# A two-layer graph network on one core: the inverse transform moved into the group in front, the state difference kept in h's tile, the aggregation in four tiles of the array

## The chip, the cores and the metric

The kernel runs on one core of a Trainium2 chip. The metric is the device time in microseconds of one execution, as the median of several runs. Lower is better. Beside it there is one profiled execution with a trace of every instruction; its page gives a span, which is a little shorter than the device time of that same execution.

The engines are named as in the profile: PE is TensorE (PEld its weight loads), DVE is VectorE, ACT is ScalarE, POOL is GpSimd and SP is SyncE, which here only issues DMAs. A name such as L735 is a line of the kernel file before the change.

## What is computed

The input x has 128 graphs of 128 nodes with 256 features, adj has 128 matrices of 128 x 128. All is fp32. Two layers run one after another, each on the normalized and rectified x, and each adds to x:

```python
h = jnp.maximum(_layernorm(x, axis=-1), 0.0)
x = x + _L0_gnn_ref(h, adj, ...)
h = jnp.maximum(_layernorm(x, axis=-1), 0.0)
x = x + _L1_gnn_ref(h, adj, ...)
```

Layer 0 takes h through a convolution branch (a 1x1 convolution, a convolution of 17 taps over the nodes, batch norms, and a sum with h), through a message branch, and then through a gated cell:

```python
x_conv = relu(bn2(conv2(relu(bn1(conv1(xc))))) + xc)      # xc is x transposed
x_nmp = einsum('bnm,bmd->bnd', A, relu(x @ w_msg.T + b_msg))
gi = concatenate([x_conv, x_nmp], -1) @ w_ih.T + b_ih
gh = x @ w_hh.T + b_hh
r = sigmoid(gi_r + gh_r)
z = sigmoid(gi_z + gh_z)
nn_ = tanh(gi_n + r * gh_n)
return (1.0 - z) * nn_ + z * x
```

Layer 1 works on the first 25 nodes only. For five groups of these nodes (25, 9, 7, 6 and 6 nodes, 53 rows together) it runs two graph convolutions and adds the weighted results:

```python
support = einsum('bnd,de->bne', x, W)
out = relu(einsum('bnm,bme->bne', norm_adj, support) + b)
```

## The kernel before

**Tiling.** Four graphs are a group; there are 32 groups q. Sixteen graphs, that is four groups, are a block of layer 1; there are 8 blocks. Activations of a group are kept with features on the partitions, as [128, 2, 512]: two halves of the features, four graphs of 128 nodes.

**Stages.** Up to about 680 us the first stages run: the 1x1 convolution and a Fourier transform of it (stage_a), products in the Fourier domain (stage_b, results in DRAM as yd), and beside them the message branch (early, results in DRAM as xmd). h itself also waits in DRAM, as hTd. Then stage_c handles the groups one by one: it applies the inverse Fourier transform, forms x_conv, and runs the gates. Beside stage_c, as its groups become ready, run layer 1's rows (second normalization), prepare (the normalized adjacency of a block, ac, and its transposed form r4) and block (the two graph convolutions).

**Order of the work.** The order of instructions on every engine is fixed when the program is built. Each stage is a generator that yields a cost and a delay in microseconds; Order.run picks among lanes by the cost that each has been charged, relative to its weight. Costs and delays only arrange instructions; on the chip each engine runs its own instructions in that order and waits on semaphores. Groups run two at a time in their lane, so that the tail of a group falls into the next one.

**stage_n (L677)** loads hT and xm of a group, as soon as the group two before has issued its last gate product. hT has three buffers, xm two.

**stage_c (L687), the start.** For each of two halves h of the group, 16 matmuls (L706) with four column tiles of 32 apply the inverse to yt (80 frequencies) and write pi, in ptmp; VectorE transposes pi in blocks into xi (L711); the next group's yt is requested (L713); for two feature halves VectorE multiplies xi by a scale and adds hT into xc (L716) and ScalarE adds a shift and rectifies (L719). xi shares a buffer with the later sums tc.

**The gates.** A product is written as seven smaller ones over sums and differences of halves of the weights and of the operands (th, tm and tc are the sums of hT, xm and xc, made on VectorE by L586). part (L730) issues matmuls of one product into a PSUM bank; bank (L744) takes a bank of pgat (three banks) or of ptmp (five). At the start of the gates p1, p6 and p5 are taken; their parts of hT and xm come first (L762 to L764), then p1's part of xc (L765), the copy of p1 into u2 (L766) and the sums tc (L767 to L769). Then follow three products of wh (L781 to L786), a second accumulation into p1 (L788), p6's part of tc (L791), p5's part (L796), sums of the next group (L797), and the products 6 and 3 of z (L803, L810), the second accumulation into p5 (L816), and products with wn (L828 to L853).

**The end of a group.** After the last gate product come two tanh on ScalarE (L855), and on GpSimd, for both feature halves, d = hT - r (L858), d times z (L859) and the sum with r into z (L861). d lies in the buffers of u2 and u3. After a delay of 11 us, in the next group, z is transposed (L878) and added to xt, which has been loaded from x (L809), and the result goes out (L887).

**Layer 1's aggregation.** prepare loads the adjacency of 16 graphs into aj by one DMA (L954), adds the identity (L958), normalizes, and transposes ac by a matmul with the constant e4 (L1001) into r4 (L1005). In ac, two graphs of 64 rows each lie on the 128 partitions. In block, after the dense products, turn (L1064) transposes a group's result into zt, gather (L1075) multiplies it by ac and adds a bias, and fuse (L1086) adds up the node groups. A gather call has four matmuls of 64 x 64 with 256 columns: for graph pair a and half s of the partitions, rows of half s give output rows of the same half s, all in one PSUM tile pg2 of [128, 2, 256].

Of the kernel before, what the change touches and what calls it, by code (L numbers as in the profile page):

```python
# [9 lines left out]
FP = mybir.dt.float32  # L10
AF = mybir.ActivationFunctionType
ALU = mybir.AluOpType
# [3 lines left out]
B, N, D = 128, 128, 256  # L16
# [3 lines left out]
P = 128  # L20
GB = 4
# [9 lines left out]
SB = 16  # L31
# [7 lines left out]
NR = sum(SIZES)  # L39
# [53 lines left out]
def _constants():  # L93

    row_node = [n for g in GROUPS for n in g]
    row_group = [i for i, g in enumerate(GROUPS) for _ in g]
    fwd, inv, tap = _fourier()
    parts = {
        "ident": np.eye(P),
        "mhalf": np.full((P, 8), -0.5),  # L100
        "fwd": fwd, "tap": tap, "inv": inv,
        "ones2": np.kron(np.eye(2), np.ones((RP, RP))),
        "et": np.zeros((P, 2 * RP)),
        "same": np.zeros((P, RP)),
        "diag": np.zeros((P, RP)),
        "e4": np.zeros((P, P)),
        "s2": np.zeros((P, 2 * WIDE)),
        "grp": np.zeros((P, NG)),
        "sgrp": np.zeros((P, 2 * NG)),
        "grpt": np.zeros((P, P)),  # L110
        "sel": np.zeros((P, P)),
        "emb": np.zeros((P, 12)),
    }

    roles = {0: [(2, 2, 0), (0, 0, 1), (1, 1, 0), (0, 0, 1)],
             1: [(0, 0, -1), (0, 0, 1), (1, 1, 0), (1, 1, 0)],
             2: [(1, 1, 0), (1, 1, 0), (0, 0, -1), (0, 0, 1)]}
    for j in range(GB):
        for role, factors in roles.items():
            for ch in range(3):  # L120
                k = WIDE * j + 3 * role + ch
                parts["sel"][ch, k] = 1
                parts["emb"][k] = np.array(factors).T.reshape(-1)
    for r, (n, g) in enumerate(zip(row_node, row_group)):
        for s in range(2):
            k = s * RP + r
            parts["et"][n, k] = 1
            parts["same"][k, [i for i in range(NR) if row_group[i] == g]] = 1
            parts["diag"][k, r] = 1
            for j in (s, s + 2):  # L130
                parts["e4"][k, j * WIDE + n] = 1
            parts["s2"][k, s * WIDE + n] = 1
            parts["grp"][k, g] = 1
            parts["sgrp"][k, s * NG + g] = 1
            parts["grpt"][g, k] = 1
    at, o = {}, 0
    for name, a in parts.items():
        at[name] = (o, o + a.shape[1])
        o += a.shape[1]
    return np.concatenate(list(parts.values()), 1).astype(np.float32), at  # L140
# [67 lines left out]
def kernel(ctx: ExitStack, tc: tile.TileContext, x, adj, consts, vecs, w_se, conv1_w,  # L208
# [380 lines left out]
    def some_sums(q, n):  # L589

        if q in IN:
            if q not in SUMS:
                hT, xm = IN[q]
                (th, a), (tm, b) = sums("th", q, hT), sums("tm", q, xm)
                SUMS[q] = th, tm, a + b
            while SUMS[q][2] and n != 0:
                SUMS[q][2].pop(0)()
                n = n and n - 1
# [85 lines left out]
        yield 0.0, 7.0  # L684
        IN[q] = hT, xm

    def stage_c(q):  # L687
        while not (q - 1 in G_DONE and q in IN):
            yield 0.0, 0.5
        some_sums(q, None)  # L690
        (hT, xm), (th, tm, _) = IN.pop(q), SUMS.pop(q)

        if (q, 0) not in IN2:
            load_yt(q, 0)
            load_yt(q, 1)
            yield 0.0, 6.0
        fr = LATE["co"]
        xi = fr.tile([P, 2, 512], FP, tag="tc", name=f"xi{q}")
        xc = fr.tile([P, 2, 512], FP, tag="xc", name=f"xc{q}")
        for h in range(2):  # L700
            yt = IN2.pop((q, h))
            pi = ptmp.tile([P, 2, 2, 4, WIDE], FP, tag="tmp", name=f"pi{q}_{h}")
            for n in range(4):
                o = n % 2 * WIDE
                for w in range(4):
                    nc.tensor.matmul(  # L706
                        pi[w * WIDE:(w + 1) * WIDE, :, :, n].rearrange("p k g c -> p g k c"),
                        inv[:F, o:o + WIDE],
                        yt[:, n // 2::2].rearrange("f g (k w c) -> w f g k c", k=2, w=4)[w],
                        start=True, stop=True)  # L710
            nc.vector.transpose(xi[:, :, h * D:(h + 1) * D],  # L711
                                pi.rearrange("p k g n c -> p k (g n c)"))
            load_yt(q + 1, h)  # L713
            s = slice(h * D, (h + 1) * D)
            for co in range(2):
                nc.vector.scalar_tensor_tensor(xc[:, co, s], xi[:, co, s],  # L716
                                               scl["bn2"][:, co:co + 1], hT[:, co, s],
                                               op0=ALU.mult, op1=ALU.add)
                nc.scalar.activation(xc[:, co, s], xc[:, co, s], AF.Relu,  # L719
                                     bias=sft["bn2"][:, co:co + 1])  # L720
        yield 1.8, 0.0

        wrz, wn, wh = LATE["wrz"], LATE["wn"], LATE["wh"]

# [34 lines left out]
        r1, r2 = r[:, :, :D], r[:, :, D:]  # L759
        early = [(0, hT, th), (2, xm, tm)]  # L760
        p1, p6, p5 = bank(wrz, 0), bank(wrz, 5), bank(wrz, 4)
        for ps, i in ((p1, 0), (p6, 5), (p5, 4)):  # L762
            part(ps, wrz, i, early, True, False)
            yield 1.75, 0.0  # L764
        part(p1, wrz, 0, xs[2:], False, True)  # L765
        nc.scalar.activation(u2, p1, AF.Copy)  # L766
        tcs, todo = sums("tc", q, xc)  # L767
        for operation in todo:
            operation()  # L769
        yield 0.87, 0.0  # L770
        xs, xh = [(0, hT, th), (2, xm, tm), (1, xc, tcs)], [(0, hT, th)]

        ve = fr.tile([P, 3, 1, D], FP, tag="ve", name=f"ve{q}")
# [22 lines left out]
        part(p5, wrz, 4, xs[2:], False, True)  # L796
        some_sums(q + 1, 2)  # L797
        yield 0.87, 0.0
        while q and q - 1 not in C_DONE:
            yield 0.0, 0.5  # L800
        z = fr.tile([P, 2, 512], FP, tag="z", name=f"z{q}")
# [52 lines left out]
        for dc in (1, 0):  # L854
            nc.scalar.activation(r[:, dc], r[:, dc], AF.Tanh, bias=v("b_ih", 4 + dc))  # L855

            d = fr.tile([P, 512], FP, tag=f"u{2 + dc}", name=f"d{q}_{dc}")
            nc.gpsimd.tensor_sub(d, hT[:, dc], r[:, dc])  # L858
            nc.gpsimd.tensor_mul(d, d, z[:, dc])  # L859
            pat = "p (j t n) -> p t j n"  # L860
            nc.gpsimd.tensor_add(z[:, dc].rearrange("p (t j n) -> p t j n", t=4, j=GB),  # L861
                                 d.rearrange(pat, j=GB, t=4),
                                 r[:, dc].rearrange(pat, j=GB, t=4))
# [83 lines left out]
    def prepare(blk):  # L947

        while not (blk - 1 in P_DONE and blk - 2 in {-2, *B1_DONE}):
# [1 line left out]
        pool, pool2, b1 = S["pool"], S["pool2"], S["b1"]  # L951
        ac, r4 = S["ac"][blk % 2], S["r4"][blk % 2]
        aj = pool.tile([NN, SB, NN], FP, tag="dd", name=f"aj{blk}")
        nc.sync.dma_start(out=aj, in_=adj[blk * SB:(blk + 1) * SB, :NN, :NN]  # L954
                          .rearrange("b n m -> n b m"))
        yield 0.0, 4.0

        for r, n, w in _runs():  # L958
# [43 lines left out]
                         start=True, stop=True)  # L1002
        for j in range(GB):
            s = slice(j * WIDE, (j + 1) * WIDE)
            nc.vector.tensor_copy(r4[s, :, j, :], pr4[s, :, j // 2, :NR])  # L1005
        yield 0.9, 1.0
        P_DONE.add(blk)

    def block(blk):
# [64 lines left out]

        def gather(q):  # L1075
            zt = zts[q]
            pg2 = ptmp.tile([P, 2, D], FP, tag="tmp", name=f"pg2{blk}_{q}")
            for a in range(2):
                for s in range(2):
                    rows = slice(s * RP, (s + 1) * RP)  # L1080
                    nc.tensor.matmul(pg2[rows, a], ac[rows, 2 * q + a], zt[rows, a],  # L1081
                                     start=True, stop=True)
            nc.vector.tensor_tensor(zt, pg2, b2row[:, None, :].to_broadcast([P, 2, D]), ALU.add)
            nc.scalar.activation(zt, zt, AF.Relu)

        def fuse(q):  # L1086
            zt = zts.pop(q)
            pf = ptmp.tile([P, D], FP, tag="tmp", name=f"pfu{blk}_{q}")
            for a in range(2):
                nc.tensor.matmul(pf[a * 2 * WIDE:(a + 1) * 2 * WIDE], s2w, zt[:, a],  # L1090
                                 start=True, stop=True)
            nc.vector.tensor_add(x1[:, q], x1[:, q], pf)
            b0 = blk * SB + q * GB
            if blk < NBLK - 1:
                nc.gpsimd.dma_start(out=out[b0:b0 + GB, :WIDE], in_=x1[:, q])
                return
            for j in range(GB):
                eng = nc.scalar if q == QS - 1 and j % 2 else nc.sync
                eng.dma_start(out=out[b0 + j, :WIDE], in_=x1[j * WIDE:(j + 1) * WIDE, q])

        for what, q in ((turn, 0), (turn, 1), (turn, 2), (gather, 0), (turn, 3), (gather, 1),
                        (gather, 2), (fuse, 0), (gather, 3), (fuse, 1), (fuse, 2), (fuse, 3)):
            what(q)
            if (what, q) == (gather, QS - 1):
                B1_DONE.add(blk)
            yield {turn: 0.45, gather: 0.9, fuse: 0.5}[what], 0.5
        F_DONE.add(blk)


# [70 lines left out]
```

## Time and profile before

| what | value |
|---|---|
| median of 3 runs | 2050.7 us (2047.82 to 2055.25) |
| the profiled execution, device time | 2049.36 us |
| its span | 2047.5 us |
| granted TensorE clock, mean | 0.995 |
| PE busy from 830 to 1936 us | 1098.14 of 1106.00 us |
| DVE, ACT, POOL busy in the same stretch | 754.04, 319.65, 354.70 us |
| aggregation matmuls, L1081 | 34.2 us busy, 256 instructions |
| inverse matmuls, L706 | 62.7 us busy, 2048 instructions |
| GpSimd's d, L858 | 87.2 us busy, 64 instructions |

Busy time of TensorE counts overlapping matmuls once. In lists of groups a row gives busy time, then the mean of one instruction in ns, then the idle time of the engine just before and what ended it. In a timeline a row gives the start, the duration, engine, line, operation and how many instructions were merged into it; a mark in brackets gives idle time before it and what ended that.

### The profile page before, as it was taken

The numbers are of one execution on the slowest core, as the hardware profiler recorded it, in microseconds if no ns is written. First come the engines' busy times: TensorE is split into PE (matmuls) and PEld (weight loads), VectorE is DVE, ScalarE is ACT, GpSimd is POOL, SyncE is SP. The second block draws the span as 40 slices with busy tenths as digits, with TensorE's granted clock in tenths as the row PEclk, the third lists the DMA queues.
The fourth block names the chain that finished last, engine by engine and source line by source line (L and its number), as shares of the span: only waits on it lengthen the run. The fifth ranks groups of instructions, "written<-read, shape, count | busy, mean of one in ns | idle before, by whom it ended". The sixth has DMA issues, their size and how long they took to land.

```text
span 2047.5 us, 34132 instructions
## 1 busy us (share of the span) xinstructions
PE 2006.3 (98%) x12852; PEld 1659.2 (81%) x12852; DVE 1285.1 (63%) x2775; ACT 688.5 (34%) x1547; POOL 741.3 (36%) x898
## 2 busy tenths in 40 slices
PE   7998999999999999999999999999999999999998
PEld 5667888888888888878788788878888888878875
DVE  6774445875433676757756776777567667766742
ACT  4663222454222344222222332232232323222333
POOL 3552665333655032422422233233224323233230
PEclk9999999999999999999999999999999999999999
DMA  9997788645777544431323232332332233323121
GB/s 217 295 284 229 265 267 281 191 162 185 253 256 245 152 127 131 116 108 53 87 73 91 75 84 83 101 80 76 83 88 78 76 98 90 86 78 104 39 71 52
DMA packets 190148, 281.91 MB, mean 138 GB/s; under 512 B 23626, under 2 KB 143375, under 8 KB 189983
## 3 DMA queue, kind: packets, MB, share of 16 engines
q1 hardware_dynamic: 156942, 185.46, 31.7%
q0 software_dynamic: 32656, 93.98, 14.5%
q8 instruction: 102, 1.67, 0.3%
q14 instruction: 64, 0.52, 0.1%
q10 hardware_dynamic: 384, 0.28, 0.1%
HBM read 187.34 MB, written 92.27 MB: 137 GB/s over the span
## 4 chain that ended last, share of the span: by engine, by line
PE 89%; DVE 3%; issue 3%; POOL 3%; DMA 2%; ACT 1%; SPq 0%; POOLq 0%; DVEq 0%; ACTq 0%
PE p L735 39%; PE pa L526 7%; PE pm L630 5%; PE ph L1038 5%; PE pz L1047 5%; PE pc L421 4%; PE pb L526 3%; PE pf L432 3%; PE px L656 3%; PE pi L706 3%; PE pg L1081 1%; PE pw L474 1%; PE po L878 1%; PE ph L410 1%; PE py L1021 1%
## 5 line engine op out<-in xcount | busy, mean ns | idle before, releaser
L858 POOL TENSOR_TENSOR d<-hTc,r 128x512 f32<-128x512 f32 x64 | 87.2, 1362 | 299.3 <-ACT r L855 288.7
L526 PE MATMUL pa<-wf,X 128*128 128x256 f32 x640 | 152.2, 381 | 0.0
L716 DVE SCALAR_TENSOR_TENSOR xc<-xi,s_bn,hTc 128x256 f32<-128x256 f32 x128 | 148.1, 1195 | 2.3
L558 DVE SCALAR_TENSOR_TENSOR y<-pa,kk 128x512 f32<-128x512 f32 x78 | 53.8, 690 | 151.4 <-ACT kk L557 151.4
L887 POOL DMA_DIRECT2D out<-xt x128 | 72.2, 569 | 172.5 <-DVE xt L884 169.3
L750 ACT ACTIVATE z<-z,brz 128x256 f32<-128x256 f32 x128 | 58.1, 501 | 221.3 <-DVE z L804 187.9
L735 PE MATMUL p<-tm,wrz 128*128 128x256 f32 x512 | 132.3, 381 | 0.0
L735 PE MATMUL p<-th,wrz 128*128 128x256 f32 x512 | 132.1, 380 | 0.0
L735 PE MATMUL p<-tc,wrz 128*128 128x256 f32 x512 | 131.8, 380 | 0.0
L526 PEld LDWEIGHTS pa<-wf,X 128*128 128x128 f32 x640 | 118.1, 190 | 16.2 <-issue 2.0
L630 PE MATMUL pm<-wmsg,hT 128*128 128x256 f32 x512 | 123.3, 386 | 0.0
L421 PE MATMUL pc<-c1w,hTa 128*128 128x256 f32 x512 | 121.4, 383 | 1.2 <-ACT hTa L412 1.2
L1040 ACT ACTIVATE hh<-ph,vec 128x96 f32<-128x96 f32 (+3 forms) x160 | 64.4, 403 | 147.0 <-PE ph L1038 137.8
L1038 PE MATMUL ph<-yz,w 128*128 128x96 f32 (+3 forms) x640 | 110.5, 327 | 1.9 <-issue 1.0
L719 ACT ACTIVATE xc<-xc,t_bn 128x256 f32<-128x256 f32 x128 | 64.8, 508 | 138.8 <-DVE xc L716 138.8
L630 PEld LDWEIGHTS pm<-wmsg,hT 128*128 128x128 f32 x512 | 97.3, 193 | 15.8 <-ACT kk L557 1.4
L421 PEld LDWEIGHTS pc<-c1w,hTa 128*128 128x128 f32 x512 | 94.3, 191 | 18.2 <-DVE h L424 4.8
L735 PEld LDWEIGHTS p<-tm,wrz 128*128 128x128 f32 x512 | 97.8, 191 | 13.5
L735 PE MATMUL p<-hTc,wrz 128*128 128x256 f32 x384 | 103.9, 393 | 5.0 <-ACT u L766 4.9
L735 PEld LDWEIGHTS p<-th,wrz 128*128 128x128 f32 x512 | 97.1, 190 | 13.6 <-PE p L735 0.2
L1038 PEld LDWEIGHTS ph<-yz,w 128*128 128x128 f32 x640 | 89.0, 195 | 23.3 <-issue 16.5
L1047 PE MATMUL pz<-hh,w 128*128 128x96 f32 (+3 forms) x640 | 107.3, 321 | 0.0
(200 smaller groups left out, 4566.1 us busy)
## 6 DMA issues: line engine op xcount, KB each, us to landing
wf<-wfd SPq DMA_DIRECT2D x160, 256.0 KB, 3.2
wfd<-ws POOLq DMA_DIRECT2D x64, 320.0 KB, 8.9
yd<-y POOLq DMA_DIRECT2D x80, 256.0 KB, 4.1
yt<-yd SPq DMA_DIRECT2D x64, 320.0 KB, 4.9
w<-in_W SPq DMA_DIRECT2D x40, 512.0 KB, 4.0
xa<-in_x SPq DMA_DIRECT2D x128, 128.0 KB, 5.2
hTd<-hTa POOLq DMA_DIRECT2D x32, 512.0 KB, 5.9
hT<-hTd SPq DMA_DIRECT2D x32, 512.0 KB, 6.3
```

The costliest lines, as they stand in the source:

```text
L421: nc.tensor.matmul(pc[:, i], hT[:, k, (2 * h + i) * N:(2 * h + i + 1) * N], c1w[:, k], start=(k == 0), stop=(k == 1))
L432: nc.tensor.matmul(pf[:, i, :F * NB], h1[:, 2 * h + i, k * P:(k + 1) * P], fwd, start=True, stop=True)
L526: nc.tensor.matmul(ps, xk(k), WF[f][:, k, s], start=(k == 0), stop=(k == 1))
L630: nc.tensor.matmul(pm[:, i], hT[:, k, j * N:(j + 1) * N], LATE["wmsg"][:, k], start=(k == 0), stop=(k == 1))
L716: nc.vector.scalar_tensor_tensor(xc[:, co, s], xi[:, co, s], scl["bn2"][:, co:co + 1], hT[:, co, s], op0=ALU.mult, op1=ALU.add)
L719: nc.scalar.activation(xc[:, co, s], xc[:, co, s], AF.Relu, bias=sft["bn2"][:, co:co + 1])
L735: nc.tensor.matmul(ps[:, m], w[:, i, k, m * P:(m + 1) * P], factor(i, x, t), start=first and j == 0, stop=last and j == len(n) - 1, skip_g ...
L858: nc.gpsimd.tensor_sub(d, hT[:, dc], r[:, dc])
L887: nc.gpsimd.dma_start(out=out[q * GB + j, WIDE:].rearrange("(t n) c -> n t c", n=WIDE), in_=xt[j * WIDE:(j + 1) * WIDE, 1:4])
L1038: nc.tensor.matmul(ph, w1[:, k, m * P:(m + 1) * P], yz[:, k, :, o:o + n], start=(k == 0), stop=(k == 1))
L1040: nc.scalar.activation(hh[:, m], ph, AF.Relu, bias=v("b1", g * 4 + m))
L1047: nc.tensor.matmul(pz, w2[:, g, m, cc * P:(cc + 1) * P], hs[g][:, m], start=(m == 0), stop=(m == 3))
```

## The change

Four things are changed.

1. The inverse with its transposes, sums with hT and rectifications becomes a function, convolved. stage_c of group q calls it for group q + 1, after p5's part at L796 and the sums at L797, if hT and xm of q + 1 have been requested and given their delay; a group for which that has not been done calls it at its own start. The transposes write xc itself and the sums work in place, so xi is gone; xc gets two buffers. The request for yt of group q + 2 moves with it.
2. At the start of a group, p1 takes all its parts at once, followed by the copy into u2 and the sums tc; the first parts of p6 and p5 come after these.
3. d is written into hT's own tile, in place, and no longer into the buffers of u2 and u3.
4. In the aggregation, half s of the rows now gives output half a, in an output tile of its own for each s; the bias add becomes two, one for each output. The planner's cost of a call goes from 0.9 to 0.5. So that the results come out in the same order, the adjacency is loaded by four DMAs that swap the middle two graphs of each four, and the constant e4 and the copies into r4 follow that.

```diff
-            for j in (s, s + 2):
+            for j in (2 * s, 2 * s + 1):
                 parts["e4"][k, j * WIDE + n] = 1
...
-    def stage_c(q):
-        while not (q - 1 in G_DONE and q in IN):
-            yield 0.0, 0.5
-        some_sums(q, None)
-        (hT, xm), (th, tm, _) = IN.pop(q), SUMS.pop(q)
-
-        if (q, 0) not in IN2:
-            load_yt(q, 0)
-            load_yt(q, 1)
-            yield 0.0, 6.0
-        fr = LATE["co"]
-        xi = fr.tile([P, 2, 512], FP, tag="tc", name=f"xi{q}")
-        xc = fr.tile([P, 2, 512], FP, tag="xc", name=f"xc{q}")
+    XC = {}
+
+    def convolved(q, hT):
+
+        xc = XC[q] = LATE["co"].tile([P, 2, 512], FP, tag="xc", name=f"xc{q}", bufs=2)
         for h in range(2):
             yt = IN2.pop((q, h))
...
-            nc.vector.transpose(xi[:, :, h * D:(h + 1) * D],
-                                pi.rearrange("p k g n c -> p k (g n c)"))
             load_yt(q + 1, h)
             s = slice(h * D, (h + 1) * D)
+            nc.vector.transpose(xc[:, :, s], pi.rearrange("p k g n c -> p k (g n c)"))
             for co in range(2):
-                nc.vector.scalar_tensor_tensor(xc[:, co, s], xi[:, co, s],
+                nc.vector.scalar_tensor_tensor(xc[:, co, s], xc[:, co, s],
                                                scl["bn2"][:, co:co + 1], hT[:, co, s],
                                                op0=ALU.mult, op1=ALU.add)
                 nc.scalar.activation(xc[:, co, s], xc[:, co, s], AF.Relu,
                                      bias=sft["bn2"][:, co:co + 1])
-        yield 1.8, 0.0
+
+    def stage_c(q):
+        while not (q - 1 in G_DONE and q in IN):
+            yield 0.0, 0.5
+        some_sums(q, None)
+        (hT, xm), (th, tm, _) = IN.pop(q), SUMS.pop(q)
+
+        if q == 0:
+            load_yt(q, 0)
+            load_yt(q, 1)
+            yield 0.0, 6.0
+        fr = LATE["co"]
+        if q not in XC:
+            convolved(q, hT)
+            yield 1.8, 0.0
+        xc = XC.pop(q)
...
-        for ps, i in ((p1, 0), (p6, 5), (p5, 4)):
-            part(ps, wrz, i, early, True, False)
-            yield 1.75, 0.0
-        part(p1, wrz, 0, xs[2:], False, True)
+        part(p1, wrz, 0, xs, True, True)
         nc.scalar.activation(u2, p1, AF.Copy)
         tcs, todo = sums("tc", q, xc)
         for operation in todo:
             operation()
-        yield 0.87, 0.0
+        yield 2.6, 0.0
+        for ps, i in ((p6, 5), (p5, 4)):
+            part(ps, wrz, i, early, True, False)
+            yield 1.75, 0.0
...
         part(p5, wrz, 4, xs[2:], False, True)
         some_sums(q + 1, 2)
         yield 0.87, 0.0
+        if q + 1 in IN:
+            convolved(q + 1, IN[q + 1][0])
+            yield 1.8, 0.0
...
-            d = fr.tile([P, 512], FP, tag=f"u{2 + dc}", name=f"d{q}_{dc}")
-            nc.gpsimd.tensor_sub(d, hT[:, dc], r[:, dc])
+            d = hT[:, dc]
+            nc.gpsimd.tensor_sub(d, d, r[:, dc])
             nc.gpsimd.tensor_mul(d, d, z[:, dc])
...
-        nc.sync.dma_start(out=aj, in_=adj[blk * SB:(blk + 1) * SB, :NN, :NN]
-                          .rearrange("b n m -> n b m"))
+        for i in range(GB):
+            nc.sync.dma_start(out=aj[:, i % 2 * 2 + i // 2::GB],
+                              in_=adj[blk * SB + i:(blk + 1) * SB:GB, :NN, :NN]
+                              .rearrange("b n m -> n b m"))
...
-            nc.vector.tensor_copy(r4[s, :, j, :], pr4[s, :, j // 2, :NR])
+            nc.vector.tensor_copy(r4[s, :, j % 2 * 2 + j // 2, :], pr4[s, :, j % 2, :NR])
...
-            pg2 = ptmp.tile([P, 2, D], FP, tag="tmp", name=f"pg2{blk}_{q}")
+            pg2 = [ptmp.tile([P, D], FP, tag="tmp", name=f"pg2{blk}_{q}_{s}") for s in range(2)]
             for a in range(2):
                 for s in range(2):
                     rows = slice(s * RP, (s + 1) * RP)
-                    nc.tensor.matmul(pg2[rows, a], ac[rows, 2 * q + a], zt[rows, a],
-                                     start=True, stop=True)
-            nc.vector.tensor_tensor(zt, pg2, b2row[:, None, :].to_broadcast([P, 2, D]), ALU.add)
+                    nc.tensor.matmul(pg2[s][a * RP:(a + 1) * RP], ac[rows, 2 * q + a],
+                                     zt[rows, a], start=True, stop=True)
+            for s in range(2):
+                nc.vector.tensor_add(zt[:, s], pg2[s], b2row)
             nc.scalar.activation(zt, zt, AF.Relu)
...
-            for a in range(2):
-                nc.tensor.matmul(pf[a * 2 * WIDE:(a + 1) * 2 * WIDE], s2w, zt[:, a],
+            for s in range(2):
+                nc.tensor.matmul(pf[s * 2 * WIDE:(s + 1) * 2 * WIDE], s2w, zt[:, s],
                                  start=True, stop=True)
...
-            yield {turn: 0.45, gather: 0.9, fuse: 0.5}[what], 0.5
+            yield {turn: 0.45, gather: 0.5, fuse: 0.5}[what], 0.5
```

## The prediction

> **What bounds the kernel now.** I read the page's busy times and chain first, then the waits of all engines, then TensorE's groups, then the timeline of one late group (1107 to 1143 us).
>
> ```profile
> span 2047.5 us, 34132 instructions
> ...
> PE 2006.3 (98%) x12852; PEld 1659.2 (81%) x12852; DVE 1285.1 (63%) x2775; ACT 688.5 (34%) x1547; POOL 741.3 (36%) x898
> ...
> PE 89%; DVE 3%; issue 3%; POOL 3%; DMA 2%; ACT 1%; SPq 0%; POOLq 0%; DVEq 0%; ACTq 0%
> ...
> L716 DVE SCALAR_TENSOR_TENSOR xc<-xi,s_bn,hTc 128x256 f32<-128x256 f32 x128 | 148.1, 1195 | 2.3
> ```
>
> TensorE is busy 98% of the span and is 89% of the chain. So only two things pay: less time on TensorE, and a stall of TensorE that goes. VectorE at 63% and GpSimd at 36% count only where TensorE waits for them.
>
> Waits (engine, line <- releaser: total us, times, longest):
>
> ```profile
> PEld p L735 <- ACT u L766: 11.6, 17, 2.2
> PE p L735 <- ACT u L766: 4.9, 7, 1.8
> ...
> ACT u L766 <- POOL z L861: 17.5, 17, 2.0
> ```
>
> Of the gate stage's matmuls these are the largest stall, and the timeline shows the whole of it at one group's start:
>
> ```profile
> 1109.76 2.94 DVE L716 SCALAR_TENSOR_TENSOR xc<-xi,s_bn,hTc 128x256 f32<-128x256 f32 x2
> ...
> 1115.33 1.33 POOL L861 TENSOR_TENSOR z<-d,r 128x512 f32<-128x512 f32 x1
> 1115.64 1.30 DVE L586 TENSOR_TENSOR tc<-xc 128x256 f32<-128x256 f32 x1
> 1116.69 0.60 ACT L766 ACTIVATE u<-p 128x512 f32<-128x512 f32 x1 [0.61 <-POOL z L861]
> 1117.04 0.43 DVE L586 TENSOR_TENSOR tc<-xc,tc 128x256 f32<-128x256 f32 x1
> 1117.34 0.73 PEld L735 LDWEIGHTS p<-hTc,wrz 128*128 128x128 f32 x4 [0.39 <-ACT u L766]
> ```
>
> ScalarE's copy of p1 into u2 (L766) waits until GpSimd has finished z (L861) of the group in front, because that group's d lies in the buffer of u2. TensorE may not add into p1 again before the copy.
>
> The aggregation, first the rows around one of its 32 calls, then what was in flight at three narrow moments in it:
>
> ```profile
> 1135.25 0.59 PE L735 MATMUL p<-xc,wn 128*128 128x256 f32 x2
> 1135.78 1.08 PE L1081 MATMUL pg<-zt,ac 64*64 64x256 f32 x8
> 1136.79 0.70 PE L735 MATMUL p<-tm,wn 128*128 128x256 f32 x2
> 1137.32 0.59 PE L735 MATMUL p<-tc,wn 128*128 128x256 f32 x2
> ```
>
> ```profile
> 1135.78 0.43 PE L1081 MATMUL pg<-zt,ac 64*64 64x256 f32 x2
> ...
> 1136.04 0.38 PE L1081 MATMUL pg<-zt,ac 64*64 64x256 f32 x2
> ...
> 1136.26 0.38 PE L1081 MATMUL pg<-zt,ac 64*64 64x256 f32 x2
> ```
>
> Each fp32 matmul is two instructions, so a call is 8. They run in pairs: starts at 1135.78, 1136.04 and 1136.26 have two each. A full-array instruction of 256 columns takes a step of 0.216 us (two in 0.43, from starts such as 1131.70, 1132.13). The call holds TensorE from 1135.25 + 0.43 = 1135.68 to 1137.32 - 0.43 = 1136.89, 1.21 us: four steps of 0.216 (0.86) and 0.35 of going into this shape and out of it.
>
> TensorE's groups:
>
> ```profile
> L706 PE MATMUL pi<-yt,cst 80*32 80x128 f32 x2048 | 62.7, 274 | 0.0
> ```
>
> 64 inverse instructions of 128 columns take 62.7 / 32 = 1.96 us a group; one after another at 0.108 they would take 6.9. So four column tiles, each with other data, do run at once.
>
> **What the Trainium skill says.** "TensorEngine Tiling (Array Packing)", Tile-to-Partition Mapping: in 64x64 mode there are four tiles, fixed by input and output halves. Before, the call uses the two diagonal ones (rows s to output half s); the pairs agree. Same page, Restrictions and Gotchas: different row tiles can't access one PSUM bank at a time. That is why four tiles need two outputs; the pairs above write different partition halves of one tile together, so the trace doesn't show the conflict. Same page, Key Properties: changing the mode drains TensorE; the 0.35 agrees. "GPSIMD Engine Reference", Specifications: GpSimd shares SBUF interfaces with VectorE, in contention with instructions of two SBUF inputs. The trace agrees: L716 takes 1195 ns beside GpSimd's d, the gates' L778 of the same shape 0.48 us, and the same subtraction L586 1.30 beside L861 and 0.43 after it.
>
> **The change part by part**, against the profiled execution's 2049.4 us (span 2047.5), 1.3 below the median of the runs, 2050.7.
>
> Aggregation in four tiles. Same 8 instructions, but in four tiles two steps instead of four: -0.432 us a call. Going in and out stays 0.35. Bounds: 0 if they still run in pairs, -0.43 at best. I take -0.43, since column tiles beside each other (L706) and row tiles with outputs of their own (L643, 32x128) both overlap in this trace, though the two together don't occur. The first seven blocks' 28 calls stand among other TensorE work: 28 x 0.43 = 12.1. The last block has no cover: its calls wait for ScalarE (4 copies and 4 ReLUs of some 0.6 between 2033 and 2040.4), so of 4 x 0.43 = 1.7 I take 0.7. VectorE's one add of 128x512 (0.69) becomes two of 128x256 (0.42), +0.15 a call, hidden in blocks 0 to 6; in the last, up to 4 x 0.15 is in that 0.7. A call now takes two of ptmp's five banks, so the third call meets those of the first, whose adds must be done: a turn, the second call and products of L735 stand between, over 2 us against 0.84 of adds. Cost 0; at most some 0.3 a call (9 us) if the adds come late. Sum -12.8.
>
> d in hT's tile. No instruction less. u2 and u3 are free of GpSimd, so the wait goes. Its price lies between 4.9 (matmuls idle) and 11.6 (weight loads idle, part of it under running matmuls). From consecutive matmul starts from L735 `th,wh` to `hTc,wrz`, less 0.216 each, the 32 groups lose 7.6, and the restart costs some 0.1 in about 14 of them: 9. I take 8. Next in line is the copy itself, which needs only p1; after the change p6, p5 (3.46) and h1, h6, h7 (1.3) stand between p1 and its second use, against 0.6 of copy. hT has three buffers; its next writer comes two groups on, so the longer hold costs nothing.
>
> Inverse moved. Its 64 matmuls, 2 transposes, 4 sums, 4 ReLUs and 2 yt loads a group go from the group's start to after p5 (L796) of the group in front, for 31 of 32 groups. TensorE's own time stays, with its transitions (about 0.37 a call by the same reckoning as above). At the start p1 is now done in one go, 12 x 0.216 = 2.6, and the tc sums lie in GpSimd's 8.3 us of d (1108.39 to 1116.66): up to 4 x 1.3 = 5.2, needed by the first p6 part with tc some 10 us after the start. The bank of p1 was last read by L842, five us before the group's end. In the middle, VectorE gets 2 x 0.71 + 4 x 0.48 = 3.3, behind the 2 sums of L797 (0.84): done 4.2 after the inverse begins. Its next job, L803, needs product 6, which ends at 2.1 + 2.6 = 4.7. So it is hidden by 0.5; and p5's second use (L816), which waits for L803 and L804 (1.4), comes at 4.7 + 3.0 = 7.7 against 6.1: slack 1.6. ScalarE's waits for the sums shorten. Cost 0, bounds -3 and +30 (rival D).
>
> Queues. On SP the yt loads now wait for an inverse in mid-group, not at the start; behind them stands xt, which ran only at 1126.57, nearly 19 us into the group, and W1, emitted after the inverse anyway. xm, hT and yt of the next group land long before use. aj in four DMAs: 24 more at 0.34 of SP, 8 us in all, spread over blocks prepared one ahead; GpSimd's b1 adds start up to 1 us later, hidden. Bounds 0 and +2. GpSimd's queue loses and gains nothing. The constant e4, r4's copies (L1005) and fuse keep count and size: 0.
>
> Sum: 2049.4 - 12.8 - 8 = 2028.6.
>
> **Rivals.** B: four tiles bring nothing, the calls stay in pairs or the products around them wait for VectorE for as long. For it: nothing here shows 2x2 tiles; against: both halves overlap. 2049.4 - 8 = 2041. C: the relief is larger. Against steps of 0.216 the gates' matmul starts lose some 25 us in all, 9 by the wait for d and about 7 by restarts after other shapes; 9 are left that a less crowded VectorE could win: 2020. For it: L716 is on the chain in places; against: these stalls lie mostly elsewhere in the group. D, the slower side: VectorE in mid-group. If a block's work (yz copies 0.27 to 0.58, aggregation adds, x1 sums) falls into the 1.6 of slack, L804 is late and TensorE stands before p5's second use. Each us beyond the slack is 31 us; the gain of 20.8 is gone at 0.67 beyond it, that is 2.3 us of other VectorE work in every group. At 1.0 beyond: 2060. Against it: in 1122 to 1131 VectorE has gaps of up to 1.95 us, and where block work comes in, TensorE's slack grows with it. E: the loads are not yet emitted when the middle is reached, and the inverse stays in front; the wait for d is gone all the same, and only some 2 us of waits for a late xc stay, 2031. Against it: hTc of a group is issued half a group and more ahead (1128.58 for the group after the next).
>
> **How the numbers follow.** The forecast 0.62, B 0.14, C 0.09, D 0.12, E 0.03. Likeliest time 2029; its own range is 2023 to 2035. Taking in C and B with their spread, 2020 to 2043 leaves out D and a little. What a measurement tells from no change is 0.3%, 6 us. Faster: all but D, less 0.04 for B's upper tail and for weak cases: 0.84; same 0.06; slower 0.10.
>
> **What would show it.** L1081 near 0.6 us busy a call, with four in flight; no wait of L766 for GpSimd; L716's mean near 0.5 us instead of 1195 ns; the inverse after L796. It is wrong if L1081 keeps 1.08, or if waits of TensorE for L804, L711 or L803 come in.

## The result

The changed kernel takes 2035.3 us (median of 4 runs, 2034.12 to 2036.88) against 2050.5 before; the ratio is 0.9925, with a 95% interval of 0.991 to 0.9941. It is faster by 15 us. The forecast was 2029, with a range of 2020 to 2043; its own range, without the rivals, was 2023 to 2035, and 2035.3 lies just past its end. Its profiled execution took 2034.12 us, with a span of 2032.3, 15.2 less than before.

Lines are now numbered as in the changed kernel: the gate matmuls are L741 (were L735), the inverse L698 (L706), the sum with h L707 (L716), the copy into u2 L769 (L766), the aggregation L1092 (L1081). The page of the changed kernel:

```profile
span 2032.3 us, 34053 instructions
...
PE 1989.3 (98%) x12852; PEld 1653.7 (81%) x12852; DVE 1285.2 (63%) x2807; ACT 683.8 (34%) x1547; POOL 741.2 (36%) x898
...
PE 90%; DVE 3%; issue 2%; DMA 2%; POOL 2%; ACT 1%; SPq 0%; POOLq 0%; DVEq 0%; ACTq 0%
```

TensorE still bounds the kernel at 98%, and its busy time fell by 17.0 us. VectorE's busy time is 1285.2 against 1285.1, though its sums with h have become much cheaper. The view of the xc tile tells why (duration of one in ns: minimum, median, maximum):

```profile
L707 DVE SCALAR_TENSOR_TENSOR xc<-xc,s_bn,hTc x128: 475/482/486, 686.4 to 1897.0; 128x256 f32<-128x256 f32 x128
...
L586 DVE TENSOR_TENSOR tc<-xc x64: 417/1483/1625, 689.0 to 1916.0; 128x256 f32<-128x256 f32 x64
L586 DVE TENSOR_TENSOR tc<-xc,tc x32: 425/1374/1557, 689.5 to 1914.7; 128x256 f32<-128x256 f32 x32
L586 DVE TENSOR_TENSOR tc<-tc,xc x32: 419/1483/1491, 690.2 to 1917.4; 128x256 f32<-128x256 f32 x32
```

Before, L716 had a mean of 1195 ns beside GpSimd's d and the tc sums a median of 420 after it. Now the sums with h have left that time and the tc sums have moved into it. Adding up the durations, the sums with h went from 153.0 to 61.6 us and the tc sums from 76.3 to 166.1: 91.4 won and 89.8 lost. The contention has changed its victim, and VectorE has won nothing.

The aggregation, in the group view (first line) and around one call in the timeline:

```profile
L1092 PE MATMUL pg<-zt,ac 64*64 64x256 f32 x256 | 21.2, 401 | 0.0
```

```profile
1142.01 0.59 PE L741 MATMUL p<-tc,wn 128*128 128x256 f32 x2
1142.54 0.66 PE L1092 MATMUL pg<-zt,ac 64*64 64x256 f32 x8
1143.13 0.70 PE L741 MATMUL p<-tm,wn 128*128 128x256 f32 x2
1143.66 0.59 PE L741 MATMUL p<-tc,wn 128*128 128x256 f32 x2
```

A call is 0.66 us busy instead of 1.08. By the reckoning of the prediction it holds TensorE from 1142.01 + 0.43 = 1142.44 to 1143.66 - 0.43 = 1143.23, 0.79 us instead of 1.21: two steps of 0.216 and about the same 0.35 of going in and out. At the start of the call four instructions are in flight, where it was two:

```profile
1142.54 0.45 PE L1092 MATMUL pg<-zt,ac 64*64 64x256 f32 x4
```

What the copy into u2 waits for now, and then TensorE's own waits in the gates and in block, where that copy no longer stands (line <- releaser: total us, times, longest):

```profile
ACT u L769 <- PE p L741: 41.9, 31, 1.4
...
PE p L741 <- DVE r L857: 1.8, 3, 0.8
PE p L741 <- DVE r L849: 1.5, 1, 1.5
PE py L1032 <- DVE r L1016: 1.5, 1, 1.5
PE p L741 <- DVE ve L830: 1.4, 1, 1.4
```

The stall for GpSimd's z is gone. In its place there are six short ones behind VectorE, 6.2 us in all; before, the comparable ones made 1.7 (L848) and 0.6 (L1005). The step that the forecast feared, L804 (now L813), holds up one weight load for 0.4 us and no matmul. The inverse stands in mid-group, behind p5's part, for 31 of the 32 groups, so rival E didn't come about.

**Where the remaining microseconds went.** The first inverse starts at 684.1 us, before it started at 679.5, although TensorE's instructions are in the same order up to there. So 4.6 us were lost in a part that the change doesn't touch, and the part after it is shorter by 19.8. To read a kernel's own part I use one stretch in all runs: from the start of the last product of stage_b (L526) to the start of the last matmul. Before it took 1377.7 us, now 1358.0.

One thing more has to come off. TensorE's granted clock falls to half in short windows of 3.4 or 6.8 us. How many there are, and where, differs between executions. Here is one such time in run e4 below (columns: busy time of each engine, then the granted clock, the DMA share and GB/s):

```profile
1015.00:1019.00 4.00, 4.00 (x51) 3.02 (x54) 2.04 (x7) 0.72 (x1) 2.40 (x4) 0.54 0.37 135
1019.00:1023.00 4.00, 4.00 (x33) 3.09 (x25) 3.93 (x6) 1.01 (x2) 3.84 (x4) 0.60 0.62 164
1023.00:1027.00 4.00, 4.00 (x20) 3.53 (x19) 4.00 (x3) 1.02 (x2) 3.84 (x3) 1.00 0.00 0
```

TensorE counts as fully busy in all three rows, but only some half of the clock was granted in the first two. A matmul takes twice as long there (in every trace full-array matmuls of 256 columns follow each other at 0.427 us inside these windows and at 0.216 outside), so half of each window is lost. Taking that half off is an estimate. The pair of traces that tests it is that of the kernel before, with 10.2 and 6.8 us of half clock: 1377.7 and 1376.0 us both become 1372.6. The pairs of the changed kernel and of e4 have equal amounts and agree to 0.2 us.

| kernel | stretch, us | half clock in it, us | without it, us | against before |
|---|---|---|---|---|
| before, two traces | 1377.7, 1376.0 | 10.2, 6.8 | 1372.6, 1372.6 | 0 |
| changed, two traces | 1358.0, 1357.8 | 6.8, 6.8 | 1354.6, 1354.4 | -18.1 |
| e1, four tiles alone | 1364.0 | 6.8 | 1360.6 | -12.0 |
| e2, d in hT's tile alone | 1368.7 | 6.8 | 1365.3 | -7.3 |
| e3, inverse moved, p1 in one go | 1427.3 | 20.5 | 1417.1 | +44.5 |
| e4, four tiles and d, two traces | 1360.3, 1360.3 | 17.1, 17.1 | 1351.8, 1351.7 | -20.8 |
| e5, changed, VectorE + 1.42 a group | 1377.4 | 17.1 | 1368.9 | +14.4 to changed |
| e6, changed, VectorE + 2.84 a group | 1419.9 | 17.1 | 1411.3 | +56.8 to changed |
| e7, e2 with two banks | 1368.5 | 6.8 | 1365.1 | -0.2 to e2 |
| e8, e4 with calls in pairs | 1360.7 | 20.5 | 1350.4 | -1.4 to e4 |
| e9, e8 with later adds | 1358.3 | 20.5 | 1348.1 | -3.7 to e4 |

### The profile page after: what moved, and what is told of

It reads as the page before. It is cut to its first block, busy times and chain, and to the rows that moved or that the text cites. A ratio compares the mean times of both kernels' runs of the same rounds, so it can differ in the third digit from the quotient of the medians.

```text
span 2032.3 us, 34053 instructions
## 1 busy us (share of the span) xinstructions
PE 1989.3 (98%) x12852; PEld 1653.7 (81%) x12852; DVE 1285.2 (63%) x2807; ACT 683.8 (34%) x1547; POOL 741.2 (36%) x898
## 4 chain that ended last, share of the span: by engine, by line
PE 90%; DVE 3%; issue 2%; DMA 2%; POOL 2%; ACT 1%; SPq 0%; POOLq 0%; DVEq 0%; ACTq 0%
PE p L741 41%; PE pa L526 7%; PE pm L630 5%; PE ph L1049 5%; PE pz L1058 5%; PE pc L421 4%; PE pb L526 3%; PE px L656 3%; PE pf L432 3%; PE pi L698 3%; PE po L887 1%; PE ph L410 1%; PE py L1032 1%; PE pw L474 1%; PE pse L614 1%
## 5 line engine op out<-in xcount | busy, mean ns | idle before, releaser
L867 POOL TENSOR_TENSOR hTc<-hTc,r 128x512 f32<-128x512 f32 x64 | 88.7, 1385 | 255.8 <-ACT r L864 255.8
L526 PE MATMUL pa<-wf,X 128*128 128x256 f32 x640 | 152.2, 381 | 0.0
L741 PE MATMUL p<-th,wrz 128*128 128x256 f32 x512 | 134.6, 385 | 0.0
L741 PE MATMUL p<-tc,wrz 128*128 128x256 f32 x512 | 131.5, 379 | 0.0
L741 PE MATMUL p<-tm,wrz 128*128 128x256 f32 x512 | 131.4, 379 | 0.0
L526 PEld LDWEIGHTS pa<-wf,X 128*128 128x128 f32 x640 | 118.2, 190 | 16.1 <-issue 2.0
L741 PEld LDWEIGHTS p<-th,wrz 128*128 128x128 f32 x512 | 94.6, 190 | 19.1 <-issue 7.4
L710 ACT ACTIVATE xc<-xc,t_bn 128x256 f32<-128x256 f32 x128 | 58.0, 500 | 149.2 <-DVE xc L707 149.2
L741 PEld LDWEIGHTS p<-tm,wrz 128*128 128x128 f32 x512 | 97.4, 190 | 13.1
L741 PEld LDWEIGHTS p<-tc,wrz 128*128 128x128 f32 x512 | 95.0, 190 | 11.6
L1058 PEld LDWEIGHTS pz<-hh,w 128*128 128x128 f32 x640 | 86.6, 191 | 17.7
L741 PE MATMUL p<-hTc,wrz 128*128 128x256 f32 x384 | 98.9, 380 | 0.0
```

Of the source, the lines that this page charges most:

```text
L526: nc.tensor.matmul(ps, xk(k), WF[f][:, k, s], start=(k == 0), stop=(k == 1))
L741: nc.tensor.matmul(ps[:, m], w[:, i, k, m * P:(m + 1) * P], factor(i, x, t), start=first and j == 0, stop=last and j == len(n) - 1, skip_g ...
L867: nc.gpsimd.tensor_sub(d, d, r[:, dc])
L1058: nc.tensor.matmul(pz, w2[:, g, m, cc * P:(cc + 1) * P], hs[g][:, m], start=(m == 0), stop=(m == 3))
```

## The experiments

The theory at the start was that of the prediction: the gain is four tiles plus the end of the wait for d, and the move of the inverse is worth nothing by itself. The rivals were that the move makes the gain, or that it takes part of it back.

**e1, four tiles alone.** The edit is the whole of part 4 of the change, in the kernel before; here only its matmuls:

```diff
-                    nc.tensor.matmul(pg2[rows, a], ac[rows, 2 * q + a], zt[rows, a],
-                                     start=True, stop=True)
+                    nc.tensor.matmul(pg2[s][a * RP:(a + 1) * RP], ac[rows, 2 * q + a],
+                                     zt[rows, a], start=True, stop=True)
```

> The kernel before with the aggregation in four tiles alone (with the constant, the adjacency loads and the copies that go with it). My theory: 28 covered calls at 0.43 us and a little in the last block, 12 us less than before: 2038 to 2039, and L1081's successor near 0.66 us busy a call. Rival (the saving is given back, because the products between the calls then wait for VectorE): under 6 us, 2045 or more.

Measured: 2045.77 us, ratio 0.9961 (0.9946 to 0.9975), 12.0 us less in the stretch, and a call 21.2 / 32 = 0.66 us busy. The size of the theory is right for the stretch; the whole runs, at about -8 us by the ratio with an interval of -5 to -11, lie between both theories. The early part, up to the last product of stage_b, took 667.8 us in this trace against 663.0, which hides some 5 of the 12.

**e2, d in hT's tile alone.** In the kernel before:

```diff
-            d = fr.tile([P, 512], FP, tag=f"u{2 + dc}", name=f"d{q}_{dc}")
-            nc.gpsimd.tensor_sub(d, hT[:, dc], r[:, dc])
+            d = hT[:, dc]
+            nc.gpsimd.tensor_sub(d, d, r[:, dc])
```

> The kernel before with d in hT's tile alone; the inverse stays at the group's start. My theory: the wait of the copy into u2 for GpSimd goes and TensorE's stall behind it, 7 to 9 us less: 2041.5 to 2043.5. Rival (the wait is only hidden by the moved inverse and the reordered p1, and with the inverse in front the sums tc or xc are late at the same place): 0 to 3 us less, 2047.5 or more.

Measured: 2046.47 us, ratio 0.9972 (0.996 to 0.9984), 7.3 us less in the stretch. What is left of the copy's waits in e2, where the numbering is that of before:

```profile
ACT u L766 <- PE p L735: 17.9, 19, 3.2
...
PEld p L735 <- ACT u L766: 2.2, 1, 2.2
...
PE p L735 <- ACT u L766: 1.8, 1, 1.8
```

ScalarE now waits for TensorE alone, and TensorE waits for the copy once instead of seven times. The inverse needn't move for that. In whole runs the gain is some 6 us by the ratio, with an interval of 3 to 8, which again lies between the two theories; in this trace the early part (669.2) hides most of the gain.

**e3, the inverse moved, with p1 in one go** (parts 1 and 2 of the change); d still lies in the buffers of u2 and u3, and the aggregation is as before.

> The kernel before with the inverse moved and p1 made in one go, d still in the buffers of u2 and u3, aggregation as before. My theory: the copy into u2 now comes due some 2.6 us after the group's start but GpSimd's z ends only about 9 us after it, and TensorE needs p1 again at about 7.4: a stall of some 2 us in each of 31 groups, up to 65 us in all, less where a block's work lies between: 2080 to 2115. Rival (the move itself frees TensorE, since VectorE's sums no longer meet GpSimd): 2040 to 2050.

Measured: 2106.52 us, ratio 1.0266 (1.0233 to 1.03), 44.5 us more in the stretch. The waits of e3, and one group's start in its timeline:

```profile
ACT u L769 <- POOL z L870: 218.5, 31, 7.8
...
PEld p L741 <- ACT u L769: 54.1, 28, 2.8
...
PE p L741 <- ACT u L769: 42.4, 24, 2.4
```

```profile
1174.16 1.26 POOL L870 TENSOR_TENSOR z<-d,r 128x512 f32<-128x512 f32 x1
1175.45 0.60 ACT L769 ACTIVATE u<-p 128x512 f32<-128x512 f32 x1 [7.49 <-POOL z L870]
1176.10 0.73 PEld L741 LDWEIGHTS p<-hTc,wrz 128*128 128x128 f32 x4 [2.84 <-ACT u L769]
1176.10 1.13 PE L741 MATMUL p<-hTc,wrz 128*128 128x256 f32 x4 [2.44 <-ACT u L769]
```

ScalarE stands 7.49 us for GpSimd's z, and TensorE 2.44 for ScalarE. Before, the inverse and the first parts of p6 and p5 lay between the end of d's group and the copy; with the inverse gone and p1 first, the wait for d is in full view in 31 of 32 groups. So the third part of the change is the condition for the first two, and the move made without it is a loss. No run separates the move of the inverse from the new order of p1.

**e4, four tiles and d, no move.**

> Four tiles and d in hT's tile, the inverse left at the group's start with the old order of p1, p6 and p5. My theory: the two gains add up and the move is worth nothing by itself: within 3 us of the changed kernel, 2030 to 2036. Rival 1 (the move costs, by stalls behind VectorE in mid-group): 4 to 8 us faster than the changed kernel, 2027 to 2031. Rival 2 (the move is what takes the stall at the start away): 2038 or more.

Measured: 2034.14 us, ratio 0.9904 (0.9889 to 0.9919). The same kernel was run a second time, with this expectation:

> Four tiles and d in hT's tile once more, on the same chip as e9. My theory: the stretch 1351.8 us without half-clock windows, within 1 us, as before, 2.7 under the changed kernel's 1354.5; in the times of whole runs the two stay within 0.3%. Rival (the 2.7 was scatter): 1354 or more.

It gave 2037.33 us, ratio 0.9927 (0.9903 to 0.995). In the stretch both traces give 1351.8 and 1351.7: the two gains add up (12.0 + 7.3 = 19.3, measured 20.8). Of the 1.5 more some 1.0 is waits that e1 still has: TensorE's waits in the stretch come to 12.1 us there, against 11.1 before, and one of 2.83 us, at 1033.65, is for the copy into u2 behind GpSimd's z. With d in hT's tile that one is gone. The changed kernel, with the move and p1's new order, takes 2.7 us more than this one without them. That lies between the theory, by which the move is worth nothing, and rival 1. In whole runs they can't be told apart, partly because e4 has 17.1 us of half clock in both traces where the changed kernel has 6.8 in both.

**before_again and after_again**, both kernels once more for their traces.

> The kernel before once more, for its trace. My theory: from the last product of stage_b to the last matmul TensorE takes the same time as in the first trace (1377.7 us) but for windows of half clock, within 1 us when half of each such window is taken off (1372.6); the time up to there differs by some us (663.0 in the first trace, up to 669.2 in others). Rival (the stretch from there on scatters by itself by several us): more than 3 us apart.

> The changed kernel once more, for its trace and more rounds. My theory: the same stretch takes 1354.6 us without the windows of half clock, within 1 us, that is 2.8 more than with four tiles and d alone (1351.8), and the same four stalls behind VectorE near 845, 848, 882 and 1012 us. Rival: the 2.8 was scatter, and the stretch now takes under 1353.

Measured: 1372.6 for the kernel before, as in the first trace, and 1354.4 for the changed one. The whole run of after_again was 2034.57 us, with a ratio of 0.9898 (0.9879 to 0.9917) on that chip. So the 2.7 us aren't scatter of the stretch, and the four stalls come again, at 845.7, 847.6, 883.0 and 1013.1 us. The early part was 664.9 us in before_again (663.0 first) and 667.6 in after_again (667.7 first); the end of the next section shows where the difference arises.

The timeline of the changed kernel shows what one of the four stalls is made of:

```profile
1008.95 3.59 POOL L970 TENSOR_TENSOR b<-aj,cst 25x400 f32<-25x400 f32 x8
...
1011.20 1.11 DVE L975 TENSOR_REDUCE dg<-b 25x16 f32<-25x400 f32 x4
...
1012.57 0.25 DVE L975 TENSOR_REDUCE dg<-b 25x16 f32<-25x96 f32 x1 [0.26 <-POOL b L970]
1012.75 0.67 DVE L826 TENSOR_TENSOR r<-u,p 128x512 f32<-128x512 f32 x1
1013.34 0.40 DVE L830 TENSOR_TENSOR ve<-ve,p 128x256 f32<-128x256 f32 x1
...
1013.80 0.70 PE L741 MATMUL p<-hTc,wh 128*128 128x256 f32 x2 [1.42 <-DVE ve L830]
```

The sums of prepare (L975) wait for GpSimd's adds of the adjacency (L970), and the gates' L826 and L830 stand behind them on VectorE. TensorE may not add into that bank again before L830 has read it. The other three stalls also fall while GpSimd makes such adds (from 844.03 and 879.59 us) or just after. The move shifted the groups against prepare, and these meetings fell badly; it is an accident of alignment in four places between 840 and 1015 us, not a cost of every group. The traces show that too: with half of the half-clock windows taken off, the distance between the changed kernel and e4 at the last gate product of a group stays at 4.86 to 4.87 us for 22 groups, from 1064 to 1880 us (4.75 to 4.76 in the second pair of traces). Some 2 us of it are the next group's inverse, which the changed kernel has then already done.

**e5 and e6, VectorE loaded in mid-group.** The changed kernel with each transpose of the inverse done twice (e5) or three times (e6):

```diff
             nc.vector.transpose(xc[:, :, s], pi.rearrange("p k g n c -> p k (g n c)"))
+            nc.vector.transpose(xc[:, :, s], pi.rearrange("p k g n c -> p k (g n c)"))
```

> The changed kernel with each transpose of the inverse done twice, 1.42 us more of VectorE in the middle of each of 31 groups; the output stays the same. My theory (slack of 1.6 us before TensorE stands): 0 to 8 us slower than the changed kernel. Rival (VectorE has no slack in mid-group): 1 us or more a group, 30 us slower.

> The changed kernel with each transpose of the inverse done three times, 2.84 us more of VectorE in mid-group. My theory: 1.2 beyond the slack, in groups without a block's work between; 15 to 38 us slower than the changed kernel, with waits of TensorE for L804's successor or for what follows it on VectorE. Rival (VectorE has far more slack): under 8 us.

Measured: e5 2049.99 us (ratio 0.9981, 0.997 to 0.9992), e6 2094.56 us (1.0194, 1.0172 to 1.0215); 14.4 and 56.8 us more in the stretch than the changed kernel. Both are dearer than the theory had it. From e5 to e6 there are 42.4 us for 31 times 1.42, that is 0.96 us for each us: beyond the slack VectorE's work is paid nearly in full. Extended back from e6, 56.8 / 31 = 1.83 of 2.84 us are paid, so the slack is about 1.0 us and not 1.6. TensorE's waits, first in e5 and then in e6, where the added lines shift the numbers by one and two (L831 and L832 are L830 above, L815 is L813, which was L804):

```profile
PE p L742 <- DVE ve L831: 9.5, 23, 2.4
```

```profile
PE p L743 <- DVE z L815: 27.7, 27, 3.0
...
PE p L743 <- DVE ve L832: 16.5, 24, 2.7
```

The forecast's place, p5's second use behind L804, decides in e6, but the slack runs out first one step later: at the bank of the fifth product of wh, whose second use waits for its first sum, L830. I hadn't reckoned that one.

**e7, two banks without four tiles.** From e2:

```diff
-                    nc.tensor.matmul(pg2[rows, a], ac[rows, 2 * q + a], zt[rows, a],
+                    nc.tensor.matmul(pg2[a][rows], ac[rows, 2 * q + a], zt[rows, a],
```

> d in hT's tile as in e2, and the aggregation with two output tiles and two bias adds, but still on the two diagonal tiles of the array (graph pair a to its own output, rows of half s to output half s), adjacency and constant as before. It tells the array tiles from the banks. My theory (four array tiles make the gain): a call keeps 1.08 us busy, and from the last product of stage_b to the last matmul TensorE takes what e2 took without half-clock windows, 1365.3 us, up to 2 us more. Rival (separate PSUM banks make the calls fast): 0.66 us a call and 1354 or less.

Measured: 2045.09 us (one run alone), 1365.1 in the stretch, 0.2 under e2. The calls in e7:

```profile
L1081 PE MATMUL pg<-zt,ac 64*64 64x256 f32 x256 | 34.2, 388 | 0.0
```

They keep 34.2 us. The second bank and the second bias add cost nothing and bring nothing; the four places in the array bring the gain. Four places with a single output were not tried, so whether they need two outputs, as the forecast has it, no run shows.

**e8 and e9, an attempt at less than both.** e4 with the second and third aggregation call, and the second and third fuse, in one step each; e9 also raises a delay in prepare:

```diff
-        for what, q in ((turn, 0), (turn, 1), (turn, 2), (gather, 0), (turn, 3), (gather, 1),
-                        (gather, 2), (fuse, 0), (gather, 3), (fuse, 1), (fuse, 2), (fuse, 3)):
+        for steps in (((turn, 0),), ((turn, 1),), ((turn, 2),), ((gather, 0),), ((turn, 3),),
+                      ((gather, 1), (gather, 2)), ((fuse, 0),), ((gather, 3),),
+                      ((fuse, 1), (fuse, 2)), ((fuse, 3),)):
...
-        yield 0.0, 7.0
+        yield 0.0, 12.0
```

> Four tiles and d in hT's tile with the inverse at the start (e4), and in addition the second and third aggregation call of a block, and its second and third fuse, each issued back to back. It is meant to beat both kernels. My theory: going into an array shape and out of it costs 0.35 us a time, two are saved in each of 7 blocks, 5 us: the stretch 1346 to 1348 without half-clock windows (e4: 1351.8), 2026 to 2031. Rival (the pairs then wait for VectorE's adds or ScalarE's ReLU): 1351 or more.

> e8 with the delay that the planner gives the adjacency's adds raised from 7 to 12 us, so that the first matmuls of prepare are issued later. e8 lost 4.1 us where the last block's matmuls waited for GpSimd's adds, which stood behind d of the last group. My theory: that stall goes and what merging saved is left, the stretch 1345.5 to 1348 without half-clock windows. Rival (the stall moves to another block, or the later prepare holds up the block): 1350 or more.

Measured: e8 2035.49 us (ratio 0.9924, 0.9903 to 0.9945), 1350.4 in the stretch; e9 2032.97 us (0.9908, 0.989 to 0.9926), 1348.1. e8 is neither within its theory nor at its rival. There most of the saving was lost at one place, where the last block's matmuls waited for GpSimd's adds, which stood behind the last group's d:

```profile
PE pa L972 <- POOL b L961: 3.9, 1, 3.9
```

e9 removes that and other short waits come up elsewhere (1.8 us at 879 us, behind L848); 3.7 us under e4 is left in the stretch, just short of what was expected. In whole runs e9, e4 and the changed kernel overlap, so e9 isn't shown to be the faster one; both e8 and e9 have 20.5 us of half clock in the stretch, against 6.8 in the changed kernel.

## Why the prediction was right, and where its sizes were off

The time alone, 2035.3, lies midway between the forecast's 2029 and rival B's 2041. What tells the two apart is the call, and e1.

- **Four tiles: right.** Forecast -12.8, measured -12.0 alone (e1). The step that the trace before didn't show, row and column tiles together, does what each does apart: 0.66 us busy a call, and 0.79 held, with the 0.35 of switching about as before. Rival B (nothing from four tiles) is out, and e7 shows that it isn't the banks.
- **d in hT's tile: right.** Forecast -8 between 4.9 and 11.6, measured -7.3 alone (e2).
- **Inverse moved, "cost 0, bounds -3 and +30": the term that was mis-sized.** It measures +2.7 us, together with p1's new order (changed against e4). The working of "hidden by 0.5" and "slack 1.6" took p5's second use as the first bank to come due; e5 shows that it is the bank behind L830, and e6 that the slack is about 1.0. At the measured load the slack just holds in ordinary groups and fails four times where prepare stands on VectorE as well. Rival D thus named the right kind of wait, but at the wrong bank, and its price is met in e6: 0.96 us for each us beyond the slack. The changed kernel stays short of the point from which it decides.
- **Relief of VectorE (rival C): didn't come about.** The cheaper sums with h were named in the forecast, as were the dearer tc sums; that they cancel was not. VectorE's busy time is 1285.2 against 1285.1, so what a less crowded VectorE would win remains untested.
- **The sum.** -20.8 was forecast for the whole; e4, which leaves out the move and p1's new order, has -20.8 in the stretch, and the changed kernel -18.1. That the first two figures are equal is luck: the parts measured alone make 19.3. Against the profiled executions the rest of the way to -15.2 is the early part, 4.6 us longer up to the first inverse, less 1.7 for 3.4 us fewer of half clock in the stretch. Taken together: -18.1 - 1.7 + 4.6 = -15.2. The forecast had no term for either. That 2035.3 still lies within 2020 to 2043 it owes to the width that was added for rivals B and C, which weren't what happened.

The early part can be followed to one place. After stage_a TensorE stands until the first load of hT for the message branch has landed; L614 uses it first. The first line is from the kernel before, the second from the changed one:

```profile
167.51 1.08 PE L614 MATMUL pse<-hT,wse 128*32 128x128 f32 x16 [6.30 <-DMA hT<-hTd]
```

```profile
172.34 1.08 PE L614 MATMUL pse<-hT,wse 128*32 128x128 f32 x16 [7.78 <-DMA hT<-hTd]
```

In the fourteen traces this product starts between 167.0 and 174.0 us. From there to the last product of stage_b it is always 494.7 to 495.5 us, or 497.0 to 497.8 in the six traces that have a window of half clock between 373 and 379 us. So the 4.6 us stand in the moment at which this product can start, 4.8 us later in the changed kernel's first trace. It doesn't go with the kernel: e5 and e6, whose TensorE order up to there is that of the changed kernel, start it at 169.3 and 169.2 us and have an early part of 664.4 and 664.7. Why the load comes earlier or later, no run tells; SyncE issued it at 164.1 us in the one trace and at 167.9 in the other.

## What to carry to other kernels

Small matmuls that use only the diagonal of the array's tiles leave half of it idle. Giving each half of the rows an output of its own and crossing the halves took a call of 1.21 us to 0.79, of which 0.35 is the change of shape, so calls of one shape belong together (e9 won 3.7 us by two such pairs in a block, less the waits that came up). When work is moved off the start of a stage, ask what it was covering there: here the inverse and the first parts of p6 and p5 hid a wait for a shared buffer that cost 45 us once it was exposed. And work put into the middle of a stage is hidden only up to the first bank that comes due for reuse, which is not always the one that the moved work stands next to.

## What the runs showed that I had not expected

TensorE's clock was granted by half in windows of 3.4 and 6.8 us even in stretches where TensorE was busy throughout. There were 6.8 to 20.5 us of them in the stretch, 3.4 to 10.2 us of time. Some come again at the same place: e4 has those near 899, 1015, 1637 and 1964 us in both traces, while the kernel before shares only the one near 1453 and the changed kernel only the one near 1641. With half of them taken off, traces of one kernel agree to 0.2 us in 1350, so differences of 2 us could be read from single traces where medians of whole runs, most with intervals of 4 to 10 us, could not tell them apart.

Moving VectorE's work out of GpSimd's time brought it nothing, because as much other work moved in. The same sum of 128x256 takes 0.42 us alone and 1.48 beside GpSimd's two-input operations, and the scaled sum 0.48 and 1.48. VectorE bears nearly all of this: in the changed kernel GpSimd's operations of 128x512 have medians of 1.27 us with no such sum beside them and of 1.33 to 1.45 with one.
